# First attention's loads, mask looks and projections put in another order; last attention's preparation taken into the second layer's FFN

## The chip, the cores and the metric

The kernel runs on one core of one Trainium2 chip, in one launch. The metric is the device time in microseconds (us). Three runs of the kernel before took 1833.39, 1827.76 and 1833.9 us, with a median of 1833.39 us.

Five engines work side by side, each through its own list of instructions, and wait for one another by semaphores. PE (TensorE) does the matmuls, and PEld stands for its weight loads. DVE (VectorE), ACT (ScalarE) and POOL (GpSimd) work element by element. SP (SyncE) issues most of the DMA transfers. Matmuls write to PSUM, the accumulator memory; everything else lies in SBUF, the on-chip memory, or in DRAM.

## The reference, cut to what matters

Four layers, each a cross attention and a feed-forward network (FFN), are added one after the other to `x` (2048 rows of 256). All attentions read the same context (1601 rows of 256).

```python
sim  = q @ k.T * 64**-0.5                      # layer 0: 8 heads of 64
x = x + softmax(sim) @ v @ Wo + bo             # q from layernorm(x), k and v from ctx
x = x + routed_experts(layernorm(x))           # 8 experts, Sinkhorn gates, top-256 tokens each
x = x + masked_attention1(layernorm(x), ctx, mask_BxSxS2)      # 1 head of 256
x = x + ternary_bitlinear_relu2_ffn(layernorm(x))
x = x + attention2(layernorm(x), ctx)                          # 1 head of 256, with biases
h = gelu(rmsnorm(layernorm(x)) @ ternary(w_up).T)              # layer 2's FFN
x = x + rmsnorm(h) @ ternary(w_down).T
x = x + masked_attention3(layernorm(x), ctx, mask_1x1xSxS2)    # 16 heads of 16
x = x + gelu_experts3(layernorm(x))                            # 8 experts by position
```

Both masks have one row pattern: for every query the first 1201 or more context columns hold a 0 and the remaining ones a 1 (where that changes is drawn), and all rows of a mask are equal. The kernel must not take that for granted. It *looks*: each of the 2 x 16 mask tiles of 128 rows is read in full, and a flag is added up if anything differs. If no flag is set, a shorter path is taken in which attentions 1 and 3 use only the last 400 context rows. In these inputs the shorter path runs.

## The kernel before, in words

**Tiling.** `x` lies in SBUF as 16 tiles of 128 rows; four tiles make a chunk `c` of 512 queries. The context is transposed once into `ctxT` (`load_context`, L120–135), which ACT copies out of PSUM.

**First attention (`attention0`, L302–520).** SP issues the 16 loads of `x` (in `__init__`, L68–71), then `Wk`, `Wv`, `Wq`, `Wo`. The keys are projected (L335–343: four head pairs by four pieces, each copied by ACT in float32 and by DVE in bfloat16), then the values (L344–355: 13 tiles of 128 context rows). The attention itself runs over 16 units, a unit being a chunk and a pair of heads. Each unit needs a preparation, the generator `prepare` (L358): the chunk's layernorm (`norm`, for the first pair of a chunk only), the projection of q, then for every query the largest score over all keys. For these maxima PE multiplies in bfloat16 (L380) into a PSUM buffer of 512 columns and DVE reduces it (L385); 24 such, and a short rest of 65 columns (L391, L396). The maxima are transposed (L406) and later subtracted inside the score matmuls (L458). In the PSUM pool `pm` three buffers serve all of this in turn.

Within a unit, 13 key tiles are walked in groups of two: score matmuls (L458, L460), an exponential on ACT (L465), value matmuls one group later (L472), and on POOL a running sum of the exponentials (L479, L481: 128 x 1024 additions in SBUF). Between them, step by step, go the preparation of the next unit (`step(nxt, 1)`) and the finish of the one before (`step(done, 1)`: a matmul with ones, L414, a copy, four reciprocals, L422, and a product, L424).

**The order.** In this part PE alone has a written order (`manual_schedule(engines={PE})`): its instructions stand as the program writes them. DVE, ACT, POOL and SP are ordered by a scheduler, which is free to move work that depends on nothing far ahead.

**The looks (`look_at_masks`, L251–299).** One step of the generator is one look: ACT squares the first 1201 columns and accumulates a flag (L291), DVE compares the last 400 with row 0 (`scalar_tensor_tensor`, L293, which accumulates a flag too), and the tile for two looks later is loaded, as a `head` and a `tail`. The program steps it once after unit 0 and twice in each unit from 1 on (`g in (3, 5)`), what is left at the end. The scheduler moves all of it ahead: in the trace the looks lie between 30 and 130 us.

**Second layer's FFN (`ffn2`, L1511–1589)** runs 16 slots (four chunks by four pieces of the hidden width), each an up projection in split precision (L1530), gelu on ACT, its square, a split of the result (`parts`, ACT and DVE) and, two slots later, the down projection (L1449). Here PE, ACT, DVE and POOL all have the written order. At the end of every slot it takes one step of `beside`, which is the preparation of the last attention (`attention3_keys`, L1860–1936: weights transposed, keys, values, then layernorm, two q projections and casts once the first chunk of `x` is final).

**Last attention (`attention3_tail`, L1938).** Units of four heads and 512 queries. Six pairs of calls of `maxima` (L1961 on PE: two heads of 400 columns; L1965 on DVE: one reduction over both) and one `shift` (transposes and an addition) stand ahead of the first slot; then each slot computes scores (L1980), exponentials (L1987), values and the maxima of six slots later.

Of the kernel before, what the change touches and what calls it, by code (L numbers as in the profile page):

```python
# [15 lines left out]
P = 128  # L16
# [20 lines left out]
def rows_of(kt):  # L37
    return min(P, NCTX - kt * P)


def drain(gen):
    if gen is not None:
        for _ in gen:
            pass


def step(gen, n):
    if gen is None:
        return
    for _ in range(n):  # L50
        if next(gen, True):
            return


class Net:


    def __init__(self, ctx, tc, a, out):
        self.tc, self.nc, self.a, self.out = tc, tc.nc, a, out
        nc = self.nc  # L60
        self.const = ctx.enter_context(tc.tile_pool(name="const", bufs=1))
        self.small = ctx.enter_context(tc.tile_pool(name="small", bufs=4))
        self.wraw = ctx.enter_context(tc.tile_pool(name="wraw", bufs=3))
        self.xnp = ctx.enter_context(tc.tile_pool(name="xnp", bufs=2))


        self.x = []
        for t in range(NT):  # L68
            xt = self.const.tile([P, D], F32, name=f"x{t}")
            nc.sync.dma_start(xt, a["x"][0, t * P : (t + 1) * P, :])  # L70
            self.x.append(xt)

# [178 lines left out]
    def look_at_masks(self, pool, names):  # L251

        nc = self.nc
        odd = pool.tile([P, len(names) * (2 * NT + 1)], F32, name="odd", bufs=1)
        self.rows = {}
        col = 0

        def flag():  # L260
            nonlocal col
            col += 1
            return odd[:, col - 1 : col]

        todo, loaded = [], []
        for k, n in enumerate(names):
            m = self.a[n].rearrange("b s k -> (b s) k") if n.startswith("mask_B") else self.a[n].rearrange("a b s k -> (a b s) k")
            row = self.const.tile([P, NTAIL], mybir.dt.int32, name=f"mrow{k}")
            nc.sync.dma_start(row, m[0, K0:].partition_broadcast(P))
            self.rows[n] = row  # L270
            todo += [(m, t, row) for t in range(NT)]

        def load():
            m, t, row = todo.pop(0)
            head = pool.tile([P, K0], mybir.dt.int32, name="head")
            nc.sync.dma_start(head, m[t * P : (t + 1) * P, :K0])
            tail = pool.tile([P, NTAIL], mybir.dt.int32, name="tail")
            nc.sync.dma_start(tail, m[t * P : (t + 1) * P, K0:])
            loaded.append((head, tail, row))

        for _ in range(2):
            load()
        yield
        for n in names:
            seen = self.small.tile([P, 1], F32, name="seen")
            junk = pool.tile([P, NTAIL], BF16, name="junk", bufs=1)
            nc.vector.tensor_scalar(junk, self.rows[n], 0.0, 0.0, ALU.not_equal, ALU.add, accum_out=seen)
            nc.vector.tensor_scalar(flag(), seen, 0.0, None, ALU.is_equal)
        while loaded:
            head, tail, row = loaded.pop(0)  # L290
            nc.scalar.activation(head, head, AF.Square, accum_out=flag())  # L291
            junk = pool.tile([P, NTAIL], BF16, name="junk", bufs=1)
            nc.vector.scalar_tensor_tensor(junk, tail, 1.0, row, ALU.mult, ALU.not_equal, accum_out=flag())  # L293
# [8 lines left out]
    def attention0(self, look):  # L302
# [5 lines left out]
        wk, wv = (x.rearrange("p (k f) -> p k f", k=2) for x in self.weights("kv0", 1024, 1024))  # L308
        wq, wo = self.weights("qo0", 1024, 1024)
        wq = wq.rearrange("p (k f) -> p k f", k=2)  # L310
        wo = wo.rearrange("p (k f) -> p k f", k=4)
        for v, n in ((wk, "Wk"), (wv, "Wv"), (wq, "Wq"), (wo, "Wo")):
            nc.sync.dma_start(v, a[f"L0_xattn_{n}"].rearrange("(k p) f -> p k f", p=P))
        with ExitStack() as s:
            self.banks(s, m=3, a=1)
            kv = s.enter_context(tc.tile_pool(name="kv0", bufs=1))
# [17 lines left out]
            for hp in range(HP):  # L334
                for k0, n in PIECES:  # L335
# [8 lines left out]
            for kt in range(NKT):  # L344
                r = rows_of(kt)
                ps = self.pm()
                for kc in range(2):
                    nc.tensor.matmul(
                        ps[:r, :], lhsT=self.ctxT[:, kc, kt * P : kt * P + r], rhs=wv[:, kc, :],
                        start=kc == 0, stop=kc == 1,  # L350
                    )
                if kt % 2:
                    nc.vector.tensor_copy(v[:r, kt, :], ps[:r, :])
                else:
                    nc.scalar.copy(v[:r, kt, :], ps[:r, :])

            xnTs = {}

            def prepare(c, hp, made):
# [78 lines left out]

            units = [(c, hp) for c in range(NCH) for hp in range(HP)]
            made = []  # L440
            s.enter_context(tc.manual_schedule(engines={mybir.EngineType.PE}))
            drain(prepare(*units[0], made))
            attn = done = None
            for u, (c, hp) in enumerate(units):
                nxt = prepare(*units[u + 1], made) if u + 1 < len(units) else None
# [39 lines left out]
                for g, kts in enumerate(groups):  # L485
                    for kt in kts:
                        scores(kt)
                        step(nxt, 1)
                        if g >= 2:
                            step(done, 1)  # L490
                    for kt in late:
                        values(kt)
                    late = kts
                    if u and g in (3, 5):
                        step(look, 1)
                    if g:
                        step(nxt, 1)
# [1013 lines left out]
    def ffn2(self, beside=None):  # L1511
# [5 lines left out]
        with ExitStack() as s:  # L1517
# [36 lines left out]
            for n in range(len(slots) + 2):  # L1554
# [5 lines left out]
                if n < len(slots):  # L1560
                    c, f = slots[n]
                    ps = up(c, f)
                    h = tp.tile([P, 2, CH], F32, name="h2")
                    nc.scalar.activation(h, ps, AF.Gelu)
                    late.append((c, f, self.parts(hp, h)))
# [10 lines left out]
                if n >= 2:  # L1576
# [4 lines left out]
                    if f == NF - 2:  # L1581
# [4 lines left out]
                                ALU.mult, ALU.add,  # L1586
                            )
                        self.ready = c + 1
                step(beside, 1)


    def attention3(self, room):
# [218 lines left out]
    def attention3_keys(self, mask, s, room):  # L1811
# [116 lines left out]
        xn = []  # L1928
        yield from self.norm_steps(0, xn)
        xnT[0] = xn[0]  # L1930
        for n in range(2):
            yield
            project(n)
        yield
        for u in range(2):
            cast(u)

    def attention3_tail(self):  # L1938
        tc, nc = self.tc, self.nc
# [2 lines left out]
        with ExitStack() as s:  # L1942
# [285 lines left out]
```

## Time and profile before

| | us |
|---|---|
| runs: median, lowest, highest | 1833.39, 1827.76, 1833.9 |
| profiled execution, its own time | 1826.28 |
| its span, first to last instruction | 1824.2 |
| mean granted TensorE clock | 0.976 |
| busy in the span: PE / DVE / ACT / POOL | 1699.6 / 909.8 / 728.5 / 690.8 |
| K projection (L338), steady run of matmuls | 25.47 to 46.31 |
| V projection starts; unit 0's first scores | 46.31; 95.72 |
| unit 0's last value matmul ends; copies of unit 0's and unit 1's sums | 143.99; 144.10 and 179.36 (35.26 apart) |
| L481 on POOL, mean of 176 | 2.378 |
| L385 on DVE, mean of 384 | 0.680 |
| ahead of the last attention's scores | 1447.95 to 1461.56 |

How to read the lines that follow. A row of the timeline has the start in us, the busy time in us, the engine, the line of the kernel, the operation, the output `<-` the inputs, the tile's partitions x elements, and how many instructions are put together (x6). A bracket at the end holds how long the engine had sat idle before and what ended that wait. A row by stretches has the stretch, its length, the busy time of each engine with its number of instructions, the clock that TensorE was granted (1.00 is full), the share of the DMA engines' time, and GB/s. A float32 matmul leaves two records in the trace.

### The profile page before, as it was taken

The numbers are of one execution on the slowest core, as the hardware profiler recorded it, in microseconds if no ns is written. First come the engines' busy times: TensorE is split into PE (matmuls) and PEld (weight loads), VectorE is DVE, ScalarE is ACT, GpSimd is POOL, SyncE is SP. The second block draws the span as 40 slices with busy tenths as digits, with TensorE's granted clock in tenths as the row PEclk, the third lists the DMA queues.
The fourth block names the chain that finished last, engine by engine and source line by source line (L and its number), as shares of the span: only waits on it lengthen the run. The fifth ranks groups of instructions, "written<-read, shape, count | busy, mean of one in ns | idle before, by whom it ended". The sixth has DMA issues, their size and how long they took to land.

```text
span 1824.2 us, 21267 instructions
## 1 busy us (share of the span) xinstructions
PE 1699.6 (93%) x8102; PEld 848.0 (46%) x8102; DVE 909.8 (50%) x1737; ACT 728.5 (40%) x963; POOL 690.8 (38%) x477
## 2 busy tenths in 40 slices
PE   6879999999999998999999999999988789999898
PEld 3323334333333334444457863664576622332687
DVE  4664565555664543662844643422045567786300
ACT  3554443453443442223234522111135456666222
POOL 2047886876887683002202730100026400211210
PEclk9889999999999998999999999999989889999999
DMA  8870000000000000454300010000000001010651
GB/s 271 280 229 1 1 1 1 1 1 1 1 1 1 1 0 12 163 220 173 111 13 1 1 32 1 1 1 0 0 1 1 13 13 21 17 22 13 221 184 39
DMA packets 52461, 94.11 MB, mean 52 GB/s; under 512 B 10093, under 2 KB 37374, under 8 KB 51454
## 3 DMA queue, kind: packets, MB, share of 16 engines
q1 hardware_dynamic: 49776, 88.92, 14.8%
q0 software_dynamic: 768, 2.10, 0.4%
q10 hardware_dynamic: 1806, 1.64, 0.3%
q8 instruction: 66, 1.08, 0.2%
q14 instruction: 45, 0.37, 0.1%
HBM read 69.30 MB, written 19.01 MB: 48 GB/s over the span
## 4 chain that ended last, share of the span: by engine, by line
PE 72%; DVE 12%; ACT 5%; DMA 4%; POOL 3%; issue 3%; SPq 0%; ACTq 0%; DVEq 0%; POOLq 0%
PE pa L472 8%; PE psc L460 6%; PE pa L557 6%; PE psc L1058 5%; PE pa L1078 5%; PE psc L1980 4%; DVE mp L385 4%; PE pa L2143 3%; PE psc L2132 3%; DVE ri L422 3%; PE pa L1449 2%; PE psc L458 2%; ACT p L1987 2%; PE pm L380 2%; PE pm L431 2%
## 5 line engine op out<-in xcount | busy, mean ns | idle before, releaser
L481 POOL TENSOR_TENSOR sp<-sp,p 128x1024 f32<-128x1024 f32 (+1 forms) x176 | 418.5, 2378 | 57.7 <-ACT p L465 47.0
L385 DVE TENSOR_REDUCE mp<-pm 128x1 f32<-128x512 f32 x384 | 242.8, 680 | 159.7 <-PE pm L380 159.0
L465 ACT ACTIVATE p<-psc 128x1024 f32<-128x1024 f32 (+1 forms) x208 | 212.9, 1024 | 260.5 <-PE psc L460 166.9
L460 PE MATMUL psc<-qT,kT 64*128 64x512 f32 (+1 forms) x832 | 221.6, 594 | 0.0
L472 PE MATMUL pa<-p,v 128*64 128x512 f32 (+1 forms) x832 | 202.3, 608 | 0.0
L1987 ACT ACTIVATE p<-psc 100x1024 f32<-100x1024 f32 x128 | 124.4, 1021 | 62.7 <-PE psc L1980 54.7
L1965 DVE TENSOR_REDUCE ms<-psc 128x2 bf16<-128x800 f32 x128 | 124.2, 988 | 46.0 <-PE psc L1961 43.4
L380 PE MATMUL pm<-kb,qb 64*128 64x512 bf16 x384 | 100.5, 389 | 27.5 <-DVE mp L385 26.0
L557 PE MATMUL pa<-w_e,xe 128*128 128x512 f32 x256 | 118.7, 614 | 0.0
L472 PEld LDWEIGHTS pa<-p,v 128*64 128x64 f32 (+1 forms) x832 | 50.9, 137 | 129.8 <-issue 126.8
L1058 PE MATMUL psc<-q,kT 128*128 128x512 f32 (+1 forms) x208 | 102.2, 610 | 0.0
L171 DVE TENSOR_SCALAR xn<-x,mv,rstd 128x256 f32<-128x256 f32 x128 | 58.2, 512 | 87.7 <-PE pm L185 52.2
L156 POOL TENSOR_SCALAR rstd<-mv 128x4 f32<-128x4 f32 x32 | 9.8, 308 | 228.6 <-DVE mv L152 185.2
L1078 PE MATMUL pa<-v,p 128*128 128x257 f32 (+1 forms) x416 | 95.3, 382 | 0.0
L460 PEld LDWEIGHTS psc<-qT,kT 64*128 64x128 f32 (+1 forms) x832 | 86.0, 185 | 19.5 <-issue 6.3
L1980 PE MATMUL psc<-q,kT 32*100 32x512 f32 x512 | 82.0, 653 | 13.2 <-ACT p L1987 11.5
L458 PE MATMUL psc<-sh,negz 64*128 64x512 bf16 (+1 forms) x416 | 87.7, 384 | 2.1 <-ACT sh L407 2.0
L1030 DVE TENSOR_REDUCE mp<-pm 128x1 f32<-128x512 f32 x64 | 34.4, 571 | 102.5 <-PE pm L1025 102.2
L1078 PEld LDWEIGHTS pa<-v,p 128*128 128x128 f32 (+1 forms) x416 | 77.5, 190 | 11.8 <-issue 0.2
L567 ACT COPY y<-pa 128x512 f32<-128x512 f32 x64 | 37.6, 587 | 96.6 <-PE pa L557 94.3
L557 PEld LDWEIGHTS pa<-w_e,xe 128*128 128x128 f32 x256 | 48.0, 194 | 55.6 <-issue 52.3
L479 POOL TENSOR_TENSOR sp<-p,p 128x1024 f32<-128x1024 f32 x16 | 37.7, 2354 | 89.4 <-ACT p L465 89.4
(376 smaller groups left out, 2730.2 us busy)
## 6 DMA issues: line engine op xcount, KB each, us to landing
table<-y SPq DMA_DIRECT2D x32, 512.0 KB, 3.2
w<-in_L_ffn_w_dram SPq DMA_DIRECT2D x16, 1024.0 KB, 6.2
head<-in_mask_BxSxS_ik_dram SPq DMA_DIRECT2D x16, 600.5 KB, 4.0
head<-in_mask_1x1xSxS_ik_dram SPq DMA_DIRECT2D x16, 600.5 KB, 4.0
bc<-turned SPq DMA_DIRECT2D x7, 1024.0 KB, 7.0
tail<-in_mask_BxSxS_ik_dram SPq DMA_DIRECT2D x16, 200.0 KB, 4.1
tail<-in_mask_1x1xSxS_ik_dram SPq DMA_DIRECT2D x16, 200.0 KB, 3.6
x<-in_x_dram SPq DMA_DIRECT2D x16, 128.0 KB, 4.0
```

The source lines that it names most:

```text
L380: nc.tensor.matmul(pair[j][:, :wd], lhsT=qb[h, i * P : (i + 1) * P], rhs=kb[h, hp, k0 : k0 + wd], start=True, stop=True,)
L385: nc.vector.tensor_reduce(mp[:, i, j, n : n + 1], pair[j][:, :wd], AX.X, ALU.max)
L460: nc.tensor.matmul(sc[:r, j, :], lhsT=kT[h, hp, kt * P : kt * P + r], rhs=q[h, :], start=False, stop=True,)
L465: nc.scalar.activation(p[:r], sc[:r], AF.Exp, scale=DH**-0.5)
L472: nc.tensor.matmul(acc[h, :], lhsT=v[:r, kt, hp * P + h.start : hp * P + h.stop], rhs=p[:r, j, :], start=kt == 0, stop=kt == NKT - 1,)
L481: nc.gpsimd.tensor_tensor(sums[:r], sums[:r], p[:r], ALU.add)
L557: nc.tensor.matmul(ps, lhsT=xnT[t // TPC][:, kc, (t % TPC) * P : (t % TPC + 1) * P], rhs=ew[kc][:, 2 * h : 2 * h + 2, :], start=kc == 0, s ...
L1058: nc.tensor.matmul(sc[:r, j, :], lhsT=kT[:, kc, ks], rhs=q[:, kc, :], start=kc == 0, stop=False)
L1078: nc.tensor.matmul(acc[:, : D + 1], lhsT=p[:r, kt, i * P : (i + 1) * P], rhs=v[:r, kt, :], start=kt == 0, stop=kt == NKT - 1,)
L1965: nc.vector.tensor_reduce(ms[u % 2][:, i, 64 * k + DH : 64 * k + 64 : 32], ps[:, :, :NTAIL], AX.X, ALU.max)
L1980: nc.tensor.matmul(sc[j // 2][:TR, j % 2, :], lhsT=kT[h, g, kt * TR : (kt + 1) * TR], rhs=q[u][h, :], start=True, stop=True,)
L1987: nc.scalar.activation(p[:TR], sc[k][:TR], AF.Exp, scale=DH**-0.5)
```

## The change: what it does

1. `__init__` only allocates the tiles of `x`. A new `weights0` issues the load of `Wk` before everything else; `attention0` loads `Wv`, then the 16 tiles of `x`, then `Wq` and `Wo`.
2. A look loads one tile `both` of 128 x 1601 instead of two. DVE's comparison multiplies by `one`, a column that ACT copies after its own part of the look, instead of the literal 1.0, so that DVE's part cannot stand ahead of ACT's. ACT joins PE in the written order of `attention0`. The steps of the looks are at `g in (1, 3, 5)` in each unit from 1 on: three looks in each of units 1 to 10, two in unit 11.
3. The V projection comes after the definition of `prepare` and is interleaved with the preparation of unit 0: one or two steps of it after each V tile.
4. `ffn2` takes an extra step of `beside` before the gelu in slots 0 to 2 and two steps at the end of slots 0 to 3.
5. The end of `attention3_keys` is cut into more steps, and now also computes the maxima of the last attention's first unit, one head at a time in PSUM buffers of `pm` (two there): 16 matmuls and 16 reductions in four steps. `attention3_tail` begins with `shift(0)` alone; its first two slots take four calls of `maxima` more.

By the order of instructions in the changed kernel, PE's work from the V projection on is: V tiles 0 and 1, eight transposes of the layernormed chunk, V2, the q projection, V3, then two pairs of maxima after each of V4 to V9, the 65-column rest, V10, the transposes of the maxima, V11, V12 and unit 0's scores. On DVE, within a steady unit, the first look stands after the first four reductions, the second after sixteen, the third after the last one. In `ffn2` the preparation's weight transposes, keys and values now stand among the first four slots, and the four steps of maxima in slots 14 to 17.

```diff
         for t in range(NT):
-            xt = self.const.tile([P, D], F32, name=f"x{t}")
-            nc.sync.dma_start(xt, a["x"][0, t * P : (t + 1) * P, :])
-            self.x.append(xt)
+            self.x.append(self.const.tile([P, D], F32, name=f"x{t}"))
...
-            head = pool.tile([P, K0], mybir.dt.int32, name="head")
-            nc.sync.dma_start(head, m[t * P : (t + 1) * P, :K0])
-            tail = pool.tile([P, NTAIL], mybir.dt.int32, name="tail")
-            nc.sync.dma_start(tail, m[t * P : (t + 1) * P, K0:])
-            loaded.append((head, tail, row))
+            both = pool.tile([P, NCTX], mybir.dt.int32, name="both")
+            nc.sync.dma_start(both, m[t * P : (t + 1) * P, :])
+            loaded.append((both[:, :K0], both[:, K0:], row))
...
             nc.scalar.activation(head, head, AF.Square, accum_out=flag())
+
+            one = self.small.tile([P, 1], F32, name="one")
+            nc.scalar.copy(one, self.ones[:, 0:1])
             junk = pool.tile([P, NTAIL], BF16, name="junk", bufs=1)
-            nc.vector.scalar_tensor_tensor(junk, tail, 1.0, row, ALU.mult, ALU.not_equal, accum_out=flag())
+            nc.vector.scalar_tensor_tensor(junk, tail, one, row, ALU.mult, ALU.not_equal, accum_out=flag())
...
+    def weights0(self):
+        wkv = self.weights("kv0", 1024, 1024)
+        self.nc.sync.dma_start(
+            wkv[0].rearrange("p (k f) -> p k f", k=2), self.a["L0_xattn_Wk"].rearrange("(k p) f -> p k f", p=P)
+        )
+        return wkv
...
-        for v, n in ((wk, "Wk"), (wv, "Wv"), (wq, "Wq"), (wo, "Wo")):
+        for v, n in ((wv, "Wv"), (wq, "Wq"), (wo, "Wo")):
             nc.sync.dma_start(v, a[f"L0_xattn_{n}"].rearrange("(k p) f -> p k f", p=P))
+            if n == "Wv":
+                for t in range(NT):
+                    nc.sync.dma_start(self.x[t], a["x"][0, t * P : (t + 1) * P, :])
...
-            s.enter_context(tc.manual_schedule(engines={mybir.EngineType.PE}))
-            drain(prepare(*units[0], made))
+            s.enter_context(tc.manual_schedule(engines={mybir.EngineType.PE, mybir.EngineType.Activation}))
+
+            first = prepare(*units[0], made)
+            for kt in range(NKT):
...
+                if kt:
+                    step(first, 2 if kt > 1 else 1)
+            drain(first)
...
-                    if u and g in (3, 5):
+                    if u and g in (1, 3, 5):
                         step(look, 1)
...
                     ps = up(c, f)
+                    if n < 3:
+                        step(beside, 1)
...
-                step(beside, 1)
+
+                step(beside, 2 if n < 4 else 1)
...
-        for n in range(2):
+        yield
+        project(0)
+        yield
+        yield
+        project(1)
+        cast(0)
+        yield
+
+        for i in range(TPC):
+            for j in range(4):
+                h = slice(32 * j, 32 * j + 32)
+                ps = self.pm()
+                nc.tensor.matmul(
+                    ps[:, :NTAIL], lhsT=qb[0][h, i * P : (i + 1) * P], rhs=kb[h, 0, :], start=True, stop=True,
+                )
+                at = 32 * j + DH
+                nc.vector.tensor_reduce(ms[0][:, i, at : at + 1], ps[:, :NTAIL], AX.X, ALU.max)
+            if i == 1:
+                cast(1)
             yield
-            project(n)
-        yield
-        for u in range(2):
-            cast(u)
...
-            for n in range(6):
-                maxima(n, 0)
-                maxima(n, 1)
-                if n == TPC - 1:
-                    shift(0)
+            shift(0)
...
-                maxima(n + 6, 0)
+                if n < 2:
+                    maxima(2 * n + 4, 0)
+                    maxima(2 * n + 4, 1)
+                maxima(n + 6 if n else 5, 0)
                 if last is not None:
                     values(*last)
                 last = (u, kt)
-                maxima(n + 6, 1)
+                maxima(n + 6 if n else 5, 1)
...
+    wkv = net.weights0()
     net.load_context()
...
-        net.attention0(net.look_at_masks(pool, masks))
+        net.attention0(net.look_at_masks(pool, masks), wkv)
```

More of the change, by code (lines that the diff above doesn't have):

```diff
@@ L299, in look_at_masks, with attention0 @@
         nc.vector.tensor_scalar(self.some, self.some, 0.0, None, ALU.is_gt)
-    def attention0(self, look):
+    def weights0(self):
[4 more added lines that the diff above has]
+        return wkv
+    def attention0(self, look, wkv):
         tc, nc, a = self.tc, self.nc, self.a
@@ L307, in attention0 @@
         halves = [slice(0, DH), slice(DH, P)]
-        wk, wv = (x.rearrange("p (k f) -> p k f", k=2) for x in self.weights("kv0", 1024, 1024))
+        wk, wv = (x.rearrange("p (k f) -> p k f", k=2) for x in wkv)
         wq, wo = self.weights("qo0", 1024, 1024)
@@ L343, in attention0 @@
                     nc.vector.tensor_copy(kb[:, hp, k0 : k0 + n], ps[:, :n])
[L344 to L355, printed above, removed]
             xnTs = {}
@@ L440, in attention0 @@
             made = []
-            s.enter_context(tc.manual_schedule(engines={mybir.EngineType.PE}))
-            drain(prepare(*units[0], made))
+            s.enter_context(tc.manual_schedule(engines={mybir.EngineType.PE, mybir.EngineType.Activation}))
+            first = prepare(*units[0], made)
+            for kt in range(NKT):
+                r = rows_of(kt)
+                ps = self.pm()
+                for kc in range(2):
+                    nc.tensor.matmul(
+                        ps[:r, :], lhsT=self.ctxT[:, kc, kt * P : kt * P + r], rhs=wv[:, kc, :],
+                        start=kc == 0, stop=kc == 1,
+                    )
+                if kt % 2:
+                    nc.vector.tensor_copy(v[:r, kt, :], ps[:r, :])
+                else:
+                    nc.scalar.copy(v[:r, kt, :], ps[:r, :])
+                if kt:
+                    step(first, 2 if kt > 1 else 1)
+            drain(first)
             attn = done = None
@@ L1930, in attention3_keys @@
         xnT[0] = xn[0]
-        for n in range(2):
+        yield
[8 more added lines that the diff above has]
+                h = slice(32 * j, 32 * j + 32)
+                ps = self.pm()
+                nc.tensor.matmul(
+                    ps[:, :NTAIL], lhsT=qb[0][h, i * P : (i + 1) * P], rhs=kb[h, 0, :], start=True, stop=True,
+                )
+                at = 32 * j + DH
+                nc.vector.tensor_reduce(ms[0][:, i, at : at + 1], ps[:, :NTAIL], AX.X, ALU.max)
+            if i == 1:
+                cast(1)
             yield
-            project(n)
-        yield
-        for u in range(2):
-            cast(u)
     def attention3_tail(self):
```

## The prediction

> **What bounds the kernel now.** I read the page's totals first, then the stretches of the first attention and around the last one, then the instructions in time.
>
> ```profile
> span 1824.2 us, 21267 instructions
> PE 1699.6 (93%) x8102; PEld 848.0 (46%) x8102; DVE 909.8 (50%) x1737; ACT 728.5 (40%) x963; POOL 690.8 (38%) x477
> ...
> 0.00:20.00 20.00, 4.72 (x17) 3.08 (x17) 10.16 (x41) 3.53 (x5) 7.20 (x20) 1.00 0.81 246
> 20.00:46.30 26.30, 26.30 (x75) 13.47 (x76) 11.74 (x30) 14.40 (x29) 2.77 (x4) 1.00 0.85 294
> 46.30:72.00 25.70, 23.51 (x61) 10.23 (x59) 10.24 (x28) 15.36 (x27) 0.07 (x1) 1.00 0.81 268
> 72.00:96.00 24.00, 15.76 (x42) 4.27 (x44) 19.39 (x38) 12.87 (x22) 3.24 (x4) 0.67 0.85 287
> 96.00:144.10 48.10, 39.57 (x172) 14.37 (x172) 30.06 (x57) 27.15 (x36) 27.65 (x12) 0.88 0.60 190
> 144.10:179.36 35.26, 33.98 (x176) 11.81 (x176) 19.87 (x32) 16.04 (x18) 28.41 (x13) 1.00 0.00 1
> 1440.00:1476.00 36.00, 26.03 (x130) 10.80 (x128) 20.89 (x28) 9.66 (x12) 8.29 (x9) 0.67 0.07 16
> ```
>
> Columns: stretch, length, busy PE, PEld, DVE, ACT, POOL, granted clock, DMA share, GB/s. PE sets the pace (93%), so only its holes can be won. They lie in 0–20 (start), 72–96 (maxima of unit 0; clock 0.67), 96–144 (unit 0: 48.1 us against 35.26 for the same work in unit 1) and 1440–1476 (ahead of the last attention). From 144 on DMA does nothing: all 32 looks at the masks are over by 130 us. In a steady unit POOL adds for 28.4 of 35.26 us.
>
> The timeline shows a look on DVE (L293), POOL's additions beside it, and unit 1, where looks are to go:
>
> ```profile
> 19.97 2.07 PE L338 MATMUL pm<-ctxT,w_kv 128*128 128x512 f32 x2 [3.48 <-DMA w_kv<-in_L_xattn_Wk_dram]
> ...
> 110.02 2.45 POOL L481 TENSOR_TENSOR sp<-sp,p 128x1024 f32<-128x1024 f32 x1 [0.18 <-ACT p L465]
> ...
> 110.32 2.59 DVE L293 SCALAR_TENSOR_TENSOR junk<-tail,mrow 128x400 bf16<-128x400 int32 x1
> 115.24 0.56 DVE L293 SCALAR_TENSOR_TENSOR junk<-tail,mrow 128x400 bf16<-128x400 int32 x1
> ...
> 151.98 9.63 POOL L481 TENSOR_TENSOR sp<-sp,p 128x1024 f32<-128x1024 f32 x4
> 153.21 2.58 DVE L385 TENSOR_REDUCE mp<-pm 128x1 f32<-128x512 f32 x4 [0.92 <-PE pm L380]
> 154.64 1.08 PE L414 MATMUL pm<-sp,ones 128*64 128x512 f32 x4 [0.18 <-DVE mp L385]
> ...
> 1450.90 0.51 PE L1961 MATMUL psc<-kb,qb 32*128 32x400 bf16 x6 [2.96 <-ACT qn L1914]
> 1461.56 2.08 PE L1980 MATMUL psc<-q,kT 32*100 32x512 f32 x6 [0.38 <-DVE ms L1965]
> ```
>
> The look begun at 110.32, 0.30 us into POOL's 2.45 us addition, ended 0.44 us after it; the one at 115.24, with POOL idle, took 0.56. All five looks that began well inside an addition behave so; the others take 0.56–0.59, but for one of 1.06. Of a steady unit's DVE work between the maxima (L385) the reciprocals (L422) read one tensor; the maxima read PSUM; only the look and one 0.68 us product read two tensors in SBUF.
>
> **The change, part by part** (against the profiled execution, 1826.3 us, span 1824.2; the median of the runs is 1833.4, the lowest 1827.8, so that the profile sits at the runs' low end).
>
> A, start. Wk no longer stands behind 16 loads of x (128 KB each) on SP's queue. K's first matmul waited 3.48 us for it, its second pair stood at 23.5 and the steady run began at 25.47. Then ACT is late next: its first transposed context is copied at 13.88 whatever Wk does, the fourth copy ended at 17.1, and K needs these. x now lands behind Wv, 2.1 MB at 250 GB/s or some 8 us later, needed first at about 45 us: covered by K's 21 us. Gain at least the 2 us that ACT's copies leave, at most 7 (all from 17.1 + 1.3 to 25.5); I take 5, because K's remaining waits are ACT's own 0.59 us copies.
>
> B, V and the first preparation. Before: V 46.31 to about 72, then norm, q and 24 maxima, ending 95.72: 49.4 us. V is 52 records of 0.43 us = 22.4 us; the preparation is bound by DVE, 24 reductions (L385, 14.44 us in the row at 76.77) plus their matmuls and 3 buffers in turn. After, PE's order puts one V tile, then two pairs of maxima. Followed with three PSUM buffers: 10.4 us for four V tiles, transposes and q; six cycles of about 3.6 us (V 1.72, 4 reductions 2.4 us partly under it) = 21.5; tail, mc and the last V tiles 6. Sum 38, gain 11.4. Ends: 8 (cycles at 4.2, if V's copies on DVE come behind all reductions) and 14 (cycles at 3.1, V fully beside them). ACT's looks, which shared this stretch (1.3 us each in the chain of waits), are gone from it.
>
> C, unit 0 without looks. Before 95.72 to 143.99 = 48.3. Its work is a steady unit's, 35.26, less the previous unit's finish (L414, 1.08) and the small waits that finish brings (0.18 + 0.25 + 0.53 + 0.33): 32.9. Gain 15.4. Ends: 17 (clock 1.00 not 0.88), 12 (a first unit with cold banks).
>
> D, looks moved into units 1 to 11, three in each (two in the last). The loads (one of 820 KB instead of two) run two looks ahead, some 24 us against 4 us to land: covered. ACT's look (1.2 us + read 0.1 + copy 0.19) comes before an exponential whose value matmuls stand a group later: covered. DVE is not. Look 1: ACT's exponential ends at 151.88, the look's flag is there at 153.45, POOL adds until 154.39; blocked as at 110.32, DVE is free at 154.83, where the maxima stood at 153.21. PE's L414 is behind them (0.18 idle already): +1.56 with 0.06 saved. Look 2 is ready 1.2 us before an addition ends; the maxima after it come 1.46 late, of which the third buffer takes about 0.36: +1.1. Look 3 falls after the last reduction, into DVE's 12.03 us of idle time: 0. (1.56 + 1.1) × 11 = 29. Low end: no blocking, looks 1 and 2 at 0.57 + 0.08 with PE late by 1.05 in all, × 11 = 11.6. High end: both wait a whole addition (the 2.59 row), 5 × 11 = 55. I take 29, by the five of five rows.
>
> The Trainium skill ("SBUF — State Buffer", section "Who interferes with whom") says that a DVE operation with two inputs in SBUF and a GpSimd operation reading SBUF exclude each other for a whole instruction, and that reductions don't contend. By it the sum is 29; by the median row of the look (576 ns) it would be 11.6, which makes the forecast 1807.
>
> E, second layer's FFN and last attention. Before the last attention 12 maxima of 0.90 us plus the 2.96 wait for ACT and 1.51 for the shift last 13.6 us (1447.95 to 1461.56). After, only the last four reductions behind the updates of x and the shift remain, about 6.2; four maxima return to the first two slots at about 0.35 net each: gain 6. In the FFN, 16 single maxima run with two PSUM buffers at 0.53 each behind DVE's 1.23 us splits; beyond the gaps there, 6.5 lost. Key and value matmuls of this preparation move to slots 0–3: they fill 5.4 us of idle PE there, but their transposed weights' copies stand on ACT behind the gelu work, a hole of 4.3 and one of 2.8 with the rest: about 0 net, ±3. Slots 5–8 lose their filler (−2), the projection fills a 1.51 us wait for POOL (+1.5). Sum −1; ends −8 (holes in full) and +7 (maxima free).
>
> On the clock, the skill's "TensorE: Matmul & The Clock Gate" (Part 1) says that after an idle window of some 3.4 us PE is granted half its clock for as long again. The rows here show clock 0.67 in 72–96 and 1440–1476, where PE was idle a third of the time; by the rule the 4.3 us hole would cost some 2 us more than its length, and the sum would be 1827.
>
> Sum: 5 + 11.4 + 15.4 − 29 − 1 = 1.8 us gained, 1824.5, rounded to 1825.
>
> **Rivals.**
> *Looks cheap* (faster). If a look costs DVE's own 0.65, D is 11.6 and the time 1826.3 − 19.2 = 1807. For it: 26 of 32 looks took 0.56–0.59. Against: they ran while POOL was idle, and POOL adds during 81% of a steady unit. It also happens if DVE's scheduler leaves the look just after an addition.
> *Looks blocked twice* (slower). Place: the look between the maxima of units 1–11; price 5 us a unit, 55 in all, 1826.3 − 32.8 + 56 = 1850. For it: 2.59 for one look, and additions end to end (four in 9.63 us), so that a look may miss the gap. Against: at 119.44 one got in between two additions. From 3.7 us a unit on (32.8 + 9 over 11, less E) the result is slower by over 0.5%.
> *Holes in the second layer's FFN* (slower). E at −12: ACT's copies and single maxima with two buffers stop PE in 16 slots by 1 us each; 1836. Against: PE has 5.4 us of idle time there that the moved work fills.
> *The start is hidden anyway*: A and half of B fall away because ACT and DVE bound them: 1835, inside the forecast's own range.
>
> **How the numbers follow.** About 0.5% (9 us) is what a measurement can tell from no change. Chances: forecast 0.40 (own range 1816 to 1834: B and C at their ends, and E ± 5), cheap 0.32, blocked twice 0.16, holes 0.12. Faster: 0.40 × 0.20 + 0.32 × 0.85 = 0.35; slower: 0.40 × 0.15 + 0.16 × 0.9 + 0.12 × 0.65 = 0.28; the rest 0.37 is the same. The range goes from the cheap case with A, B, C at good ends half in (1802) to the twice-blocked case (1848).
>
> **What would show it.** A: K's run starts at about 20, not 25.5. B: the first scores at about 79. C: unit 0 takes 33 us. D: units 1–10 take 37.9 us instead of 35.26, with L293 rows of 1 to 2.6 us; at 36.3 the cheap case, at 40 the blocked one. E: from the FFN's last down matmul to the first scores of the last attention 6 us, not 13.6, and that FFN some 7 us longer. Wrong would make me: looks with a median near 0.57 in steady units, DVE waiting for ACT's flags longer than for POOL, or PE waiting for L293 not at all.

## The result: 1.47% slower

Four runs of the changed kernel took 1855.04 to 1856.35 us, median 1855.43; before, the median of four was 1830.58 (1825.03 to 1833.9). The ratio is 1.0147, with a 95% interval of 1.0125 to 1.0168: slower, by 25 us between these medians and 27 by the ratio. Forecast were 1825 us, with a range from 1802 to 1848. The time lies outside it.

The profiled execution of the kernel after took 1856.35 us, its span is 1854.6, 30.4 us longer than before. It was the slowest of its four, and the profiled one of before, at 1826.28, lies near the low end of its own, so that the account by traces is some 5 us larger than the medians say. The same view by stretches as before (length, busy PE, PEld, DVE, ACT, POOL, granted clock, DMA share, GB/s), for the start, K, V with the first preparation, unit 0, unit 2, the second layer's FFN, what is ahead of the last attention's scores, and its first 40 us:

```profile
0.00:14.00 14.00, 3.43 (x12) 2.36 (x13) 3.47 (x16) 2.36 (x3) 3.04 (x14) 1.00 0.84 269
14.00:44.50 30.50, 27.60 (x81) 13.93 (x80) 15.01 (x46) 9.77 (x21) 6.82 (x11) 0.94 0.55 175
44.50:83.70 39.20, 34.01 (x102) 12.20 (x103) 22.59 (x39) 6.46 (x13) 2.98 (x4) 1.00 0.00 0
83.70:115.80 32.10, 32.10 (x173) 11.25 (x174) 16.33 (x27) 15.40 (x18) 25.86 (x11) 1.00 0.11 34
154.15:192.50 38.35, 34.72 (x176) 12.00 (x176) 24.02 (x38) 19.81 (x27) 29.12 (x13) 1.00 0.19 62
1350.60:1481.20 130.60, 107.15 (x528) 82.20 (x526) 57.61 (x119) 60.32 (x71) 62.59 (x60) 0.86 0.02 5
1481.20:1486.80 5.60, 1.58 (x11) 0.51 (x11) 4.31 (x9) 0.00 (x0) 1.36 (x2) 0.84 0.02 6
1486.80:1526.80 40.00, 35.39 (x200) 10.06 (x200) 23.02 (x27) 20.35 (x23) 1.23 (x2) 0.72 0.05 11
```

Two of the answering rows of before were not shown yet, the FFN and the last attention's first 40 us:

```profile
1341.40:1448.00 106.60, 93.21 (x514) 74.12 (x512) 54.54 (x107) 59.30 (x70) 61.18 (x57) 0.94 0.02 3
...
1461.60:1501.60 40.00, 35.60 (x220) 10.77 (x222) 24.10 (x28) 23.38 (x26) 1.23 (x2) 0.82 0.06 12
```

The first attention did nearly what was forecast: units 1 to 10 became 3.1 us longer (2.2 where the next unit starts a new chunk; 38.35 against 35.26 in a steady one), unit 11 5.1, units 12 to 15 not at all. The FFN became 24 us longer: 14 us more of busy PE (only 14 more records of matmuls; the clock is 0.86 instead of 0.94) and 10 us more of idle PE. Taken line by line, the matmuls of the maxima, which stood elsewhere before, are 3.0 us of the busy time. The remaining 11 us are the 512 records that the kernel before has on the same lines, run more slowly: the 256 of the down projection took 37.89 us for 33.83, the 16 of the keys 9.19 for 6.23. The down projection's row, before and after (busy PE and PEld, then the clock of the whole stretch, DMA share and GB/s):

```profile
1341.40:1448.00 106.60, 33.83 (x256) 32.70 (x256) 0.94 0.02 3
...
1350.60:1481.20 130.60, 37.89 (x256) 36.98 (x256) 0.86 0.02 5
```

PE's idle time grew by 0.9 us in the FFN's first 40 us and by 9.2 us behind them, of which 4.1 are waits of and behind the maxima. The FFN in these two parts, before and after:

```profile
1341.40:1381.40 40.00, 32.93 (x164) 25.54 (x163) 22.39 (x42) 23.77 (x31) 24.52 (x25) 0.87 0.01 1
1381.40:1448.00 66.60, 60.28 (x352) 48.59 (x350) 32.16 (x67) 35.53 (x39) 36.66 (x32) 0.97 0.02 4
...
1350.60:1390.60 40.00, 32.06 (x102) 19.13 (x100) 12.08 (x28) 15.00 (x22) 10.08 (x11) 0.74 0.01 0
1390.60:1481.20 90.60, 75.08 (x427) 63.07 (x426) 45.54 (x92) 45.31 (x49) 52.51 (x49) 0.91 0.03 7
```

The whole account, from the first and last instruction of each stage in the two traces:

| term | forecast | measured |
|---|---|---|
| A: K's last matmul ends sooner (46.3 to 44.5) | 5 gained | 1.8 gained |
| B: V and first preparation (49.4 to 39.2) | 11.4 gained | 10.2 gained |
| C: unit 0 (48.4 to 32.1) | 15.4 gained | 16.3 gained |
| D: units 1 to 15 (549.4 to 583.6) | 29 lost | 34.1 lost |
| between the first attention and the FFN | 0 | 3.4 lost |
| E: FFN (106.6 to 130.5) | about 7 lost | 23.9 lost |
| E: from there to the scores (13.6 to 5.6) | 7.4 gained | 8.0 gained |
| E: last attention (225.9 to 232.0) | 1.4 lost | 6.1 lost |
| the rest | 0 | 0.9 gained |

The 3.4 us in between lie in code that the change does not touch: 1.5 us in the first attention's last 26 records of matmuls (8.83 us for 7.33) and 1.8 in the experts' matmuls, which from first to last took 147.0 us in the profile of before, 148.8 after and 148.3 to 151.9 in those of the runs below, 151.9 in one whose first attention is that of before (`e2`). That the change has no part in these 3.4 us is likely, and not shown.

In unit 2, the timeline of after shows the look on DVE (L292), POOL's additions (L493) and the maxima (L381) behind the look:

```profile
162.03 7.42 POOL L493 TENSOR_TENSOR sp<-sp,p 128x1024 f32<-128x1024 f32 x3
163.22 1.59 DVE L292 SCALAR_TENSOR_TENSOR junk<-both,one,mrow 128x400 bf16<-128x400 int32 x1 [0.90 <-ACT one L290]
164.75 2.47 DVE L381 TENSOR_REDUCE mp<-pm 128x1 f32<-128x512 f32 x4
165.48 0.37 PE L376 MATMUL pm<-kb,qb 64*128 64x512 bf16 x1 [0.97 <-DVE mp L381]
176.94 2.35 DVE L292 SCALAR_TENSOR_TENSOR junk<-both,one,mrow 128x400 bf16<-128x400 int32 x1 [0.34 <-ACT one L290]
179.22 3.67 DVE L381 TENSOR_REDUCE mp<-pm 128x1 f32<-128x512 f32 x6
179.96 0.37 PE L376 MATMUL pm<-kb,qb 64*128 64x512 bf16 x1 [1.24 <-DVE mp L381]
188.51 0.64 DVE L292 SCALAR_TENSOR_TENSOR junk<-both,one,mrow 128x400 bf16<-128x400 int32 x1 [2.48 <-ACT one L290]
```

This is step D as the prediction put it: in this unit looks 1 and 2 take 1.59 and 2.35 us, look 3 takes 0.64, and PE waits 0.97 and 1.24 us for the maxima that stand behind.

And the FFN's first slots in the timeline of after. PE waits for ACT's copies of the transposed weights (L227, L232), which stand behind a table load and the gelu work. Later the down matmuls (L1461) wait by the view of waits: 3.1 us at 1407 and 4.9 us at 1433, in front of the second and the third chunk's first ones:

```profile
1353.00 1.28 ACT L1578 ACT_TABLE_LOAD   x1 [24.19 <-PE psc L1542]
1357.26 0.63 ACT L227 COPY w_l3k<-pm 128x256 f32<-128x256 f32 x2
1357.66 1.12 PE L223 MATMUL pm<-ident,w_l 128*128 128x128 f32 x4 [4.39 <-ACT w_l3k L227]
1366.38 3.04 PE L1894 MATMUL pm<-ctxT,w_l3k 128*128 128x400 f32 x4 [2.78 <-ACT w_l3k L232]
...
PE pa L1461 <- DVE x L1598: 4.9, 1, 4.9
PE pm L223 <- ACT w_l3k L227: 4.4, 1, 4.4
PE pm L1958 <- DVE ms L1962: 3.8, 6, 1.8
PE pa L1461 <- ACT hh L1586: 3.1, 1, 3.1
```

### The profile page after: what moved, and what is told of

It is laid out like the page before. It is cut to its first block, busy times and chain, and to the rows that moved or that the text cites. A ratio compares the mean times of both kernels' runs of the same rounds, so it can differ in the third digit from the quotient of the medians.

```text
span 1854.6 us, 21232 instructions
## 1 busy us (share of the span) xinstructions
PE 1714.5 (92%) x8102; PEld 854.7 (46%) x8102; DVE 933.7 (50%) x1745; ACT 729.9 (39%) x995; POOL 694.6 (37%) x477
## 4 chain that ended last, share of the span: by engine, by line
PE 70%; DVE 13%; ACT 6%; issue 5%; POOL 4%; DMA 1%; SPq 1%; ACTq 0%; DVEq 0%; POOLq 0%
PE psc L472 6%; PE pa L484 6%; PE psc L1070 5%; PE pa L569 5%; PE pa L1090 5%; PE psc L2009 4%; DVE mp L381 3%; PE psc L2161 3%; PE pa L2172 3%; DVE ri L418 3%; DVE junk L292 2%; ACT p L2016 2%; PE psc L470 2%; PE pa L1461 2%; PE pm L427 2%
## 5 line engine op out<-in xcount | busy, mean ns | idle before, releaser
L493 POOL TENSOR_TENSOR sp<-sp,p 128x1024 f32<-128x1024 f32 (+1 forms) x176 | 423.1, 2404 | 76.3 <-ACT p L477 67.8
L381 DVE TENSOR_REDUCE mp<-pm 128x1 f32<-128x512 f32 x384 | 240.3, 677 | 135.6 <-PE pm L376 135.0
L1994 DVE TENSOR_REDUCE ms<-psc 128x2 bf16<-128x800 f32 x120 | 116.9, 988 | 49.0 <-PE psc L1990 48.5
L169 DVE TENSOR_SCALAR xn<-x,mv,rstd 128x256 f32<-128x256 f32 x128 | 54.0, 479 | 82.8 <-PE pm L183 46.8
L470 PEld LDWEIGHTS <-negz 64*128 64x128 bf16 (+1 forms) x416 | 21.6, 94 | 113.2 <-issue 113.0
```

The source lines that it names most:

```text
L381: nc.vector.tensor_reduce(mp[:, i, j, n : n + 1], pair[j][:, :wd], AX.X, ALU.max)
L470: nc.tensor.matmul(sc[:r, j, :], lhsT=negz[h, :r], rhs=sh[h, :], start=True, stop=False)
L493: nc.gpsimd.tensor_tensor(sums[:r], sums[:r], p[:r], ALU.add)
L1994: nc.vector.tensor_reduce(ms[u % 2][:, i, 64 * k + DH : 64 * k + 64 : 32], ps[:, :, :NTAIL], AX.X, ALU.max)
```

## The experiments

Runs `e1` to `e4` were made on one chip, `e5` to `e7` on a second, `e8` and `e9` on a third, each time with the kernel before beside them (medians 1828.88, 1830.8 and 1828.06 us). The edits are cut, and shown against the changed kernel.

### Which half costs what

`e1`: in the changed kernel, `ffn2`, `attention3_keys` and `attention3_tail` are those of before.

> The changed kernel with the second layer's FFN and the last attention (items 4 and 5) put back as before; items 1 to 3 stay. The traces place 5.9 us of the loss by the end of the first attention and 9.2 us by the end of the experts, and the rest from the second layer's FFN on. Theory (two separate losses): 1826 + 9 = 1835 us, FFN of layer two back at 106.6 us. Rival (the FFN is slow because of what the first attention left, its clock or its buffers): FFN still near 130 us, total above 1845.

Measured: 1837.21 us, before 1828.88, ratio 1.0046 (1.0029 to 1.0063). The FFN took 105.6 us. Items 1 to 3 alone cost some 8 us.

`e2`: the kernel before with those three functions of after.

> The kernel before with items 4 and 5 alone. Theory: the FFN is some 24 us longer, the time ahead of the last attention's scores some 8 shorter, the last attention's first slots some 6 longer, in sum 22 slower: 1848 us. My prediction's term said 1 us slower (1827) with 8 at most (1834).

Measured: 1847.12 us, ratio 1.0086 (1.0055 to 1.0117). The FFN took 130.5 us again, the time to the scores fell to 4.3, the last attention took 229.2 instead of 225.9. The second half alone costs 16 us by the ratio and 18 by the medians, and the FFN is as long without items 1 to 3. (The profiled execution, 1853.37 us, was the slowest of five.) The term that I had put at 1 us lost, 8 at most, is the one that failed.

### What a look costs, and where

`e3`: DVE's look with one tensor in SBUF instead of two.

```diff
-            nc.vector.scalar_tensor_tensor(junk, tail, one, row, ALU.mult, ALU.not_equal, accum_out=flag())
+            nc.vector.tensor_scalar(junk, tail, one, 0.0, ALU.is_gt, ALU.add, accum_out=flag())
```

> The changed kernel, where DVE's part of a look reads the mask's tail and one column instead of tail and row 0: a tensor_scalar with the same accumulated flag, behind the same wait for ACT. It leaves out the comparison with row 0. Theory (DVE's two-input look is shut out while POOL adds): looks at 0.6 us each, steady units from 38.35 to about 36, 11 units x 2.3 = 25 us less, 1830 us. Rival (what costs is DVE standing still for ACT's flag, in front of the maxima): units stay at 37.7 or more, 1848 us or more.

Measured: 1825.61 us, 30 us less than the changed kernel, which was not run beside it; against before 0.9975 (0.9956 to 0.9994). The source view of the look and a steady unit:

```profile
L292 DVE TENSOR_SCALAR_CACHE_REDUCE junk<-both,one x32: 612/629/630, 125.6 to 515.5; 128x400 bf16<-128x400 int32 x32
...
152.31:188.09 35.78, 34.35 (x176) 11.79 (x176) 21.49 (x38) 19.80 (x27) 28.54 (x13) 1.00 0.20 67
```

All 32 looks take 0.61 to 0.63 us (min/median/max in ns ahead of the times), where the two-tensor look took 0.63 to 2.79 with a median of 1.59. They stand in the same place behind the same wait for ACT, in the midst of POOL's additions (the one begun at 174.14 took 0.63 us, with POOL adding from 170.99 to 176.05), and the unit falls from 38.35 to 35.78. So 2.57 of the 3.09 us are what the two-tensor look lost beside POOL's additions, and 0.52 are what is left: the look's own time and its wait for ACT's flag. This is what the Trainium skill ("SBUF — State Buffer", section "Who interferes with whom") says of a DVE operation with two inputs in SBUF beside a GpSimd operation that reads it, and the runs agree, down to the form with an accumulator that is said not to contend.

`e4`: `e1` with two looks per unit, both behind the last maximum.

```diff
-                    if u and g in (1, 3, 5):
+                    if g == 5 or (u == 0 and g == 3):
                         step(look, 1)
...
-                if u == 0:
-                    step(look, 1)
                 drain(done)
                 drain(nxt)
+                step(look, 1)
```

> As the run with items 1 to 3 alone, but with the looks where DVE has 12 us without work: two per unit in all 16 units, one step at g = 5 and one after the unit's last preparation step, both after the last maximum. Theory (a look costs only where the maxima stand behind it): steady units back at 35.3 us, the first attention 28 us shorter than before, total 1800 us. Rival (a look costs time wherever it is, through ACT's written order or by holding POOL up): units at 36.5 or more, total 1818 or more.

Measured: 1803.1 us, ratio 0.9846 (0.9811 to 0.988). The steady unit from its windows, and the two looks of one unit on DVE, behind its last maxima (L396):

```profile
151.80:187.05 35.25, 33.98 (x176) 11.79 (x176) 22.67 (x37) 18.56 (x25) 28.82 (x13) 1.00 0.14 47
...
217.77 0.19 DVE L396 TENSOR_REDUCE mc<-mp 128x8 f32<-128x32 f32 x1
219.24 0.63 DVE L292 SCALAR_TENSOR_TENSOR junk<-both,one,mrow 128x400 bf16<-128x400 int32 x1 [1.29 <-ACT one L290]
224.38 0.63 DVE L292 SCALAR_TENSOR_TENSOR junk<-both,one,mrow 128x400 bf16<-128x400 int32 x1 [4.50 <-ACT one L290]
```

35.25 us, the unit without looks. The looks here keep both inputs, some still take up to 2.2 us, and ACT still has them in its written order; none of it costs anything, since DVE has nothing else to do. Units 1 to 15 took 549.4 us, as before. With that, what A, B and C gained is kept whole.

### The start

In the changed kernel and in `e4` K took some 30.5 us instead of 26.3. DVE's row of after at 25.43 says why, and PE's behind it:

```profile
25.43 0.57 DVE L283 TENSOR_SCALAR_CACHE_REDUCE junk<-mrow 128x400 bf16<-128x400 int32 x1 [3.34 <-DMA mrow<-in_mask_BxSxS_ik_dram]
27.53 16.94 PE L347 MATMUL pm<-ctxT,w_kv 128*128 128x512 f32 x44 [2.90 <-DVE kb L352]
```

The scheduler puts the looks' test of a mask's first row, two instructions, ahead of DVE's copies of K, and that row's load now stands behind `x`, `Wq`, `Wo` and `bo`. `e7` is `e4` with the rows loaded after `Wv`:

```diff
             todo += [(m, t, row) for t in range(NT)]
+        yield
...
             if n == "Wv":
+                step(look, 1)
                 for t in range(NT):
```

> The run with looks in DVE's idle time, and the two masks' first rows loaded ahead of x instead of after bo. In the changed kernel DVE waits 3.3 us at 25.4 for such a row, in front of K's copies, and PE waits 2.9 us for those. Theory: that wait is what kept the start from gaining: K's projection ends 3 to 4 us sooner (at about 41.5), total 1799. Rival (K is bound by ACT's copies or by x, now 0.4 MB later): K ends at 45 as before, total 1803.

Measured: 1798.97 us, ratio 0.9839 (0.9803 to 0.9874), on another chip than `e4`. K ran from 16.1 to 42.6, without that wait and at full clock:

```profile
16.10:42.60 26.50, 26.45 (x81) 13.70 (x80) 15.09 (x48) 9.72 (x21) 7.54 (x11) 1.00 0.58 190
```

It starts 1.5 us later than in `e4` and ends 2.6 sooner. It is the best version found, 1.6% below the kernel before; the intervals of its ratio and of `e4`'s overlap, so that what it gains on `e4` rests on the traces.

### The second layer's FFN

`e5`: the kernel before with item 4 alone, the whole `ffn2` of after.

> The kernel before with item 4 alone: the second layer's FFN takes the last attention's preparation in seven more steps in its first four slots; the end of the preparation and the twelve maxima ahead of the last attention stay as before. Theory (most of the FFN's loss is the early steps: PE stands for ACT's copies of transposed weights, runs on at the low clock, and later slots have nothing left to fill their waits): FFN from 106.6 to about 120 us, the time ahead of the last attention's scores as before, 13 to 14 us, total 1840. Rival (the loss is the sixteen single-head maxima in two PSUM buffers): FFN at 108 to 110, total 1829.

Measured: 1843.82 us, ratio 1.008 (1.0055 to 1.0106). FFN 122.9 us, that is 16.3 longer with no maximum in it. The same two holes are there, 4.39 and 2.78 us, and later ones of 5.4 and 3.4. Of the 16.3 us 11.3 are idle time and 5.0 busy time. But the two early holes stand in the place of others: in its first 40 us the FFN leaves PE idle for 8.0 us here and for 7.1 in the kernel before (holes of 0.86, 2.78, 1.80 and 1.18). The added idle time stands behind them.

`e6`: items 4 and 5, but with the extra steps late.

```diff
-                    if n < 3:
-                        step(beside, 1)
...
-                step(beside, 2 if n < 4 else 1)
+                step(beside, 2 if n > 8 else 1)
```

> The kernel before with items 4 and 5, but the extra steps of the preparation are taken late: one per slot up to slot 8, two from slot 9 on, none ahead of a gelu. Weights, keys and values stay where they were before; the maxima still stand in the FFN's last slots. Theory: the FFN loses only what the maxima and the later steps cost, 7 us (about 114), the time ahead of the scores falls from 13.6 to 6, the first slots give back 4: total about 1829. Rival (maxima are the cost): FFN still at 125 or more, total 1843.

Measured: 1840.13 us, ratio 1.0056 (1.0037 to 1.0075). FFN 122.6 us: 16.0 longer, where 7 was expected, so the maxima with late steps cost as much as the early steps do without maxima. Of the two theories neither was right by itself; and as early steps with maxima (`e2`) cost 23.9 and not 32.3, the two losses do not add up.

`e8`: like `e6`, the maxima two by two.

```diff
-                    if n < 3:
+                    if n > 6:
                         step(beside, 1)
...
-                step(beside, 2 if n < 4 else 1)
+                step(beside, 1 if n < 16 else 2)
...
                 nc.vector.tensor_reduce(ms[0][:, i, at : at + 1], ps[:, :NTAIL], AX.X, ALU.max)
+                if j == 1:
+                    yield
```

> As the run with late steps, but the sixteen maxima in eight steps of two instead of four of four, one step between the up and the down matmuls of a slot and one at its end. With late steps the FFN was 16.0 us longer, and its trace shows PE waiting for reductions between the maxima of one step, 0.7 us each, and 1.9 us behind DVE's split. Theory (four maxima in a row through two PSUM buffers are what costs): FFN from 122.6 down to 116, total 1833. Rival (each maximum costs its place however it is spread, or the preparation's moved steps cost): FFN 121 or more, total 1840.

Measured: 1841.75 us, ratio 1.0076 (1.0054 to 1.0098). FFN 126.6 us: not 116, and longer than with four in a row. The theory fell. PE's two largest waits in the FFN, `e6` first and `e8` below:

```profile
PE pm L1944 <- DVE ms L1948: 6.7, 11, 1.9
PE pm L185 <- DVE xn L171: 4.9, 2, 3.1
```

```profile
PE pm L185 <- DVE xn L171: 10.7, 4, 4.3
PE pm L1540 <- DVE ms L1950: 3.4, 1, 3.4
```

The 6.7 us of waits for the maxima's reductions became 3.4, as meant, but the steps brought forward for it put the transposes of two layernorms (L185) side by side, and these wait 10.7 us for DVE's `xn` (L171) instead of 4.9; the clock is 0.87 instead of 0.90. So the experiment changed two things, and does not price the maxima by themselves.

`e9`: six early steps, from slot 2 on, one between up and down and one at the end.

```diff
-                    if n < 3:
+                    if 1 < n < 8:
                         step(beside, 1)
...
-                step(beside, 2 if n < 4 else 1)
+                step(beside, 1)
```

> As the run with item 4 alone (FFN 122.9 us), with nearly as many early steps (six for seven), but from slot 2 to 7 and one by one, between the up and the down matmuls of a slot and at its end, so that no two weights are transposed in a row before the second up. Theory (the FFN's early holes are transposes waiting for two PSUM buffers whose copies stand behind gelu work on ACT; up and down matmuls in between hide them): FFN at 114, total 1833. Rival (the loss of item 4 is the later slots' missing filler, wherever the early steps stand): FFN at 120 or more, total 1840.

Measured: 1831.93 us, ratio 1.0023 (1.0003 to 1.0042). FFN 113.0 us, 9.9 shorter than in `e5` for the same work, and 1 us from the 114 expected. The rows of `e5` and `e9`, whole and for the first 40 us:

```profile
1342.20:1465.10 122.90, 98.18 (x518) 78.23 (x519) 52.66 (x109) 60.44 (x71) 64.31 (x60) 0.92 0.03 5
1342.20:1382.20 40.00, 31.99 (x141) 21.94 (x140) 14.98 (x34) 19.35 (x28) 10.77 (x12) 0.96 0.01 1
```

```profile
1341.30:1454.30 113.00, 95.57 (x518) 77.48 (x519) 56.02 (x109) 59.81 (x71) 65.13 (x60) 0.90 0.03 5
1341.30:1381.30 40.00, 36.01 (x172) 25.98 (x171) 19.62 (x40) 23.64 (x32) 21.76 (x24) 0.96 0.01 1
```

PE's busy time differs by 2.6 us, its idle time by 7.3, of which 4.0 lie in the first 40 us. So where the early steps stand is the larger part of what item 4 costs, 9.9 of 16.3 us; that it is the transposes' holes alone is not shown, since 3.3 us of idle time went from later slots too. The other 6.4 us against before are in part later waits: behind the first 40 us PE is idle for 13.4 us, in the kernel before for 6.3. There are holes of 5.9 us at 1391 and of 3.4 at 1445, where the kernel before had none over 2.1 us past the FFN's first 20. That reading is of the trace alone; no run takes it apart.

## Why the prediction was wrong

A. The term was mis-sized, 1.8 for 5. The step that failed is "covered by K's 21 us", said of the loads that come later. It looked at who needs `x`, and not at the mask rows behind `x` on SP's queue, nor at DVE's order, in which their test stands ahead of K's copies. `e7` moves the loads of the two rows: the new wait goes, and K ends 2.6 us sooner than in `e4`. (ACT's first copy of the context came at 12.49, not at 13.88 "whatever Wk does".)

B and C. Right within 1.2 us each, by their own steps: one V tile against two pairs of maxima, three PSUM buffers, and unit 0 as a steady unit without the finish. The six cycles of one V tile and two pairs of maxima took 3.8 us on average, where 3.6 was said.

D. The mechanism was right, and is now shown: 3.09 us in a steady unit where 2.66 was said, of which 2.57 go when DVE's look reads one tensor instead of two (`e3`). The low end, looks at 0.57, was wrong as a forecast of this kernel; in `e3`, where they take 0.6, a steady unit lost 0.52 us, half of what the low end said. The sum was 5 us short, half of it because it took unit 11, which lost 5.1 us, for a steady one.

E. Here the prediction failed, by 21 us: 1 lost was said, and 22.0 were (23.9 in the FFN and 6.1 in the last attention, less 8.0 gained between them). Two of the FFN's terms held. The holes "of 4.3 and one of 2.8" came at 4.39 and 2.78 us, and "about 0 net" is 0.9 us of idle time in the first 40 us, because the 5.4 us of holes were filled as said. The "6.5 lost" for the maxima came out as 3.0 us of matmuls and 4.1 of waits, though late steps with maxima cost 16.0 (`e6`), and no run prices the maxima by themselves.

The steps that failed are two. The first and larger one put a lower clock at nothing in the sum: the same 512 records of matmuls took 11 us longer, with the granted clock at 0.86 instead of 0.94. The prediction had 2 us for that, after the 4.3 us hole, in its paragraph on the clock and outside the sum. What made the clock fall so far is not shown. The second is "slots 5–8 lose their filler (−2)" with "the projection fills a 1.51 us wait for POOL (+1.5)". The second chunk's first down matmuls, which waited for nothing before, waited 3.1 us, the third chunk's 4.9 instead of 0.7, and the wait for POOL stood there twice, at 1.48 us each. Behind the first 40 us the idle time outside the maxima grew by 5 us, where 0.5 was said.

In the last attention 4.7 of the 6.1 us are busy PE, with 8 more records of matmuls and the clock at 0.94 instead of 0.96. The end of −8 for the whole of E was passed by 14. The rival "holes in the second layer's FFN" named the right place and half the size (12 for 22), with a chance of 0.12; its mechanism, 1 us of wait in each of 16 slots, is not what came. (In the rival "looks blocked twice" the gains are 5 + 11.4 + 15.4 = 31.8 us, not 32.8; its 1850 stands.)

## What to carry to other kernels

Place work for an engine beside the critical path behind the last instruction that the critical path wants from it: here the same 32 looks cost 34 us with most of them ahead of maxima, and nothing behind the last ones. Where one engine shuts another out, as POOL's additions did DVE's looks here, price an instruction at the other's remaining time, not at its own; a form of it that reads one tensor instead of two was not held up (0.6 us in all 32 looks of `e3`). When steps are moved as filler, price the place they leave as well as the place they go to, walk the new order on every engine with its buffers, put what a lower clock adds into the sum (here 11 of 24 us), and give such a term a range as wide as the idle time on both sides.

## What was not expected of the hardware

The granted clock after the same holes was not the same. The FFN's first slots have the same instructions in the same order in the changed kernel and in `e5`, with a hole of 4.39 and one of 2.78 us. In stretches of 2 us (the clock is the third number from the end of the line, ahead of DMA share and GB/s, as in all these rows), after the second hole, the changed kernel first:

```profile
1366.60:1368.60 2.00, 2.00 (x4) 0.95 (x4) 0.00 (x0) 0.00 (x0) 1.96 (x1) 0.50 0.00 0
1372.60:1374.60 2.00, 2.00 (x4) 0.70 (x3) 0.00 (x0) 0.00 (x0) 0.00 (x0) 0.50 0.00 0
1376.60:1378.60 2.00, 2.00 (x6) 1.62 (x5) 1.36 (x5) 0.00 (x0) 0.00 (x0) 0.50 0.00 0
1378.60:1380.60 2.00, 2.00 (x7) 0.94 (x6) 0.00 (x0) 0.00 (x0) 0.00 (x0) 0.86 0.00 0
```

```profile
1350.20:1352.20 2.00, 2.00 (x6) 1.56 (x6) 0.00 (x0) 0.46 (x2) 0.00 (x0) 0.50 0.00 0
1358.20:1360.20 2.00, 2.00 (x6) 0.78 (x5) 0.00 (x0) 0.21 (x1) 1.46 (x1) 1.00 0.00 0
1362.20:1364.20 2.00, 2.00 (x9) 1.61 (x9) 1.18 (x4) 0.60 (x1) 0.00 (x0) 1.00 0.00 0
```

In the changed kernel the clock fell at both holes, and after the second one PE ran at half clock for some 12.5 us (1366.4 to 1378.9) without standing still; in `e5` it fell once, for some 3 us, and not at all at the second hole. `e2`, with the same holes, stands in between: some 3.5 us at half clock after the second one. The first four matmul records behind that hole take 3.04 us in the row of the changed kernel above and 1.61 in `e5`:

```profile
1357.47 1.61 PE L1882 MATMUL pm<-ctxT,w_l3k 128*128 128x400 f32 x4 [2.78 <-ACT w_l3k L234]
```

From there to the first down matmul the same instructions took 17.5 us in the changed kernel, 13.1 in `e2` and 11.5 in `e5`. The Trainium skill's page "TensorE: Matmul & The Clock Gate" (Part 1) speaks of a free-running window of 3.4 us, which fits that the same hole is sometimes seen and sometimes not, and of full clock after a busy window of that length, which the 12.5 us don't fit. The last attention's first 40 us, whose holes are not the same, had 0.72 after and 0.82 before. What keeps the clock low on a busy PE was not tried. So a difference of some microseconds between two runs in this stage can't be put down to the order of instructions alone.
